# Issuing the additions of x to finished batches two blocks earlier in a bidirectional WKV and binary FFN kernel

## The chip, the cores and the metric

The kernel runs on one core of one Trainium2 chip. Its time is device microseconds for one execution. The kernel before takes 489.81 us, the median of three runs (489.59 to 489.88). The core has a matrix engine (TensorE, PE in the profile, with its weight loads as PEld), a vector engine (VectorE, DVE), an activation engine (ScalarE, ACT), a general engine (GpSimd, POOL) and a queue engine (SyncE, SP) that issues most transfers. Each engine works through its own list of instructions in order; semaphores make one engine wait for another, or for a transfer.

## The reference

For four batches of 1024 time steps and 1024 channels, with `x` as the gate input and one tensor `kv` as both key and value:

```python
tf    = sigmoid(sum(time_emb))                    # one scalar per batch
decay = exp(-exp(w)) * (0.5 + 0.5 * tf)
ek, ekv = exp(min(k, 30)), exp(min(k, 30)) * k
nf, df = scan over time of (a = a*decay + ekv, b = b*decay + ek)
nb, db = the same scan in reverse
euk = exp(min(u + k, 30))
num, den = nf + nb - ekv + euk*k, df + db - ek + euk
y   = sigmoid(x) * num / max(den, 1e-8) * (0.8 + 0.2 * tf)
bw  = where(weight >= 0, 1, -1) * mean(abs(weight), axis=1)
out = x + y @ bw.T + bias
```

The last line is what this case is about: the product is 1024 by 1024 by 1024 for each batch, and `x` is added to it at the very end.

## The kernel before

The work is cut into 32 **blocks**, `g = 0 .. 31`. Block `g` is batch `g // 8` and the 128 channels `g % 8`, over all 1024 time steps, with channels on the 128 partitions (transposed there by the PE, L266 and L272). A block costs VectorE a fixed list: two scans forward (L366), two backward (L379), the numerator's terms (L350), the own terms (L356), the denominator (L389) and a Newton step with the gate (L423). GpSimd floors and clamps the denominator (L396, L346), and multiplies the quotient together (L416, L419, L428); ScalarE takes exponentials and logarithms, and splits the result in a high part (L433) whose remainder GpSimd computes (L438). The own terms are added to the numerator by an accumulating transfer that GpSimd issues (L384).

When the eight blocks of a batch are done, the batch is contracted with the signs of the weight. For batches 0 to 2 the output comes in 16 **groups** `q`, each one half of the time steps (`h`, 512 rows) and one block of 128 output channels: `q = 16 b + 8 h + oc`. A group is 16 matmuls (L449), is scaled and biased by ScalarE (L461), turned back by the PE (L469), copied to a staging tile (L557) and stored to the output in pairs of groups by SP (L135). The groups of a batch are spread over the blocks of the next batch: for batch 0, two groups in each of the blocks 9 to 16; for batches 1 and 2, from blocks 16 and 24 on, five half groups per block. The last batch is contracted differently after the last block, with its rows on the partitions, and `x` is added there by VectorE (L539, L541, L531).

So for batches 0 to 2 the stored output still lacks `x`. The function `add_x(b, n)` (L137) supplies it: GpSimd issues one transfer of 256 rows by 1024 columns (1 MB) from `x` to the output, with an addition at the destination (L140). There are four per batch, `n = 0 .. 3`. Those with `n` 0 and 1 lie in the first half of the time steps, those with `n` 2 and 3 in the second. An addition may only be issued when the four stores of its half have landed, and the framework puts semaphore waits for these stores ahead of it on GpSimd's list; it finds a wait needless for the second addition of a half.

The order of everything is written out by hand in the loop over `g`. Within one block the lines that matter are, in this order: loads by SP (L679 to L686); the denominator of the block before by VectorE, the own-numerator transfer by GpSimd, and then the additions of that block,

```python
            if g > 0:
                dve_denominator(g - 1)
                dma_own_numerator(g - 1)
            for i in adds[g]:
                add_x(*i)
```

and later GpSimd's floor (L707), its clamp (L710), the remainders (L712), `den_product` (L724), `num_product` (L750), VectorE's `dve_newton_gate` (L762, the line L423), which reads what `den_product` (L416) wrote, and GpSimd's `gated_product` (L764). In a block with an addition, ScalarE's logarithm is placed after the edge of the numerator (L721) instead of before it (L709). Additions that are due at 32 are issued behind the last block (L795).

Of the kernel before, what the change touches and what calls it, by code (L numbers as in the profile page):

```python
# [21 lines left out]
def kernel(  # L22
# [32 lines left out]
    NC = C // P  # L55
# [505 lines left out]
    steps = B * NC  # L561
# [36 lines left out]
    fill(g + 2, 0, pieces(range(q + 5, q + groups)))  # L598


    adds = {g: [] for g in range(steps + 1)}
    for b in range(B - 1):
        for n in range(NT // 2):
            adds[min((b + 2) * NC + 2 * n, steps)].append((b, n))

# [9 lines left out]
    with tc.manual_schedule():  # L617
# [57 lines left out]
        for g in range(steps):  # L675
            b, cc = divmod(g, NC)
# [163 lines left out]
        n = NT - 1  # L840
# [41 lines left out]
```

## Time and profile before

| | |
|---|---|
| median of three runs | 489.81 us |
| the profiled execution's own time | 489.83 us |
| its span in the profile | 488.0 us |
| VectorE busy | 474.9 us (97%) |
| GpSimd busy | 402.2 us (82%) |
| PE busy | 363.9 us (75%) |
| ScalarE busy | 335.9 us (69%) |
| transfers of `add_x` | 12 of 1024 KB, median 11.8 us from issue to landing |
| stores of pairs of groups | 24 of 512 KB, median 5.1 us from issue to landing |

Times in the profile count from the start of the span. In a timeline, each line gives start, duration, engine, line of the kernel, operation, what is written and read, and in brackets how long the engine stood idle before it and what ended that. The queue rows (SPq, POOLq) are instructions that a sequencer handles itself. Block `g` is taken to begin with VectorE's L389; block 14 begins at 195.26, block 16 at 222.25, block 18 at 249.30, and the last one, 31, at 425.41.

### The profile page before, as it was taken

Reading aid. Unit: us, or ns where it says so; the run is one execution under the profiler, and the core shown is the slowest. Engines: PE = TensorE matmul, PEld = TensorE weight load, DVE = VectorE, ACT = ScalarE, POOL = GpSimd, SP = SyncE. Lnnn points to the kernel's source line nnn. Section 1 sums busy time; section 2 is a strip of 40 time slices with the busy share of each in tenths; the row PEclk is TensorE's granted clock in tenths of the full one; section 3 lists DMA queues with packets and bytes.
Section 4 is the critical chain, followed back from the end, with each engine's and each line's share of the span. In section 5 each row is a group of like instructions: output and inputs, shape, how many; then the busy total and the mean of one; then the engine's idle time right before and its main releaser. Section 6 shows DMA issues by size and latency. Waiting matters only on the chain.

```text
span 488.0 us, 5214 instructions
## 1 busy us (share of the span) xinstructions
PE 363.9 (75%) x1813; PEld 296.9 (61%) x1813; DVE 474.9 (97%) x331; ACT 335.9 (69%) x466; POOL 402.2 (82%) x276
## 2 busy tenths in 40 slices
PE   3434433344588877778999998965999998989996
PEld 2333332233466666656777777744888777868885
DVE  6999999999999999999999999999999999999976
ACT  4795968869595967769697879697866979724000
POOL 3379999999999999999999999999999999991000
PEclk9975566666699999999999999985999999999999
DMA  8865565555455555559787996889569697899954
GB/s 227 246 173 146 156 174 141 137 141 140 112 147 150 147 141 139 147 139 254 177 208 161 264 235 173 167 213 221 126 108 277 151 271 213 188 229 284 235 198 176
DMA packets 89762, 89.49 MB, mean 183 GB/s; under 512 B 2660, under 2 KB 80776, under 8 KB 88200
## 3 DMA queue, kind: packets, MB, share of 16 engines
q1 hardware_dynamic: 83320, 59.78, 41.0%
q0 software_dynamic: 6400, 29.37, 31.6%
q8 instruction: 14, 0.23, 0.2%
q14 instruction: 12, 0.10, 0.1%
q10 hardware_dynamic: 16, 0.00, 0.0%
HBM read 55.59 MB, written 29.36 MB: 174 GB/s over the span
## 4 chain that ended last, share of the span: by engine, by line
DVE 75%; PE 17%; issue 3%; ACT 2%; POOL 0%; DMA 0%; SPq 0%; DVEq 0%; POOLq 0%; ACTq 0%
DVE num L379 13%; DVE den L379 13%; DVE den L366 13%; DVE num L366 12%; PE wide L517 8%; DVE den L389 7%; DVE num L350 6%; DVE den L423 6%; PE po L449 5%; DVE euk L356 4%; PE last L517 2%; PE bank L517 1%; PE sgT L272 1%; PE turned L469 1%; PE kT L266 1%
## 5 line engine op out<-in xcount | busy, mean ns | idle before, releaser
L449 PE MATMUL po<-gated,wT 128*128 128x512 f32 x768 | 199.7, 408 | 0.3 <-ACT staged L557 0.3
L449 PEld LDWEIGHTS po<-gated,wT 128*128 128x128 f32 x768 | 141.9, 192 | 30.4 <-ACT staged L557 0.8
L266 PE MATMUL kT<-ident,k_rows 128*128 128x128 f32 x248 | 42.1, 325 | 61.6 <-issue 43.0
L272 PE MATMUL sgT<-ident,sg_rows 128*128 128x128 f32 x256 | 43.2, 324 | 46.4 <-DVE den L423 41.2
L438 POOL TENSOR_TENSOR gated<-num,gated 128x512 fp32r<-128x512 f32 x60 | 75.6, 1280 | 2.4
L266 PEld LDWEIGHTS kT<-ident,k_rows 128*128 128x128 f32 x248 | 33.8, 167 | 69.4 <-issue 51.6
L379 DVE TENSOR_TENSOR_SCAN den<-bank,edge_den,den 128x1024 f32<-128x1024 f32 x32 | 74.8, 2339 | 0.4 <-ACT edge_den L372 0.4
L416 POOL TENSOR_TENSOR den<-den,eu 128x1024 f32<-128x1024 f32 x31 | 73.8, 2380 | 1.4 <-ACT eu L411 1.4
L379 DVE TENSOR_TENSOR_SCAN num<-bank,edge_num,num 128x1024 f32<-128x1024 f32 x32 | 74.8, 2337 | 0.0
L419 POOL TENSOR_TENSOR num<-num,eu 128x1024 f32<-128x1024 f32 x31 | 73.7, 2377 | 0.8 <-DMA num<-euk 0.8
L428 POOL TENSOR_TENSOR num<-den,num 128x1024 f32<-128x1024 f32 x30 | 71.8, 2393 | 2.8 <-DVE den L423 0.5
L366 DVE TENSOR_TENSOR_SCAN den<-bank,den 128x1024 f32<-128x1024 f32 x32 | 72.2, 2258 | 0.0
L366 DVE TENSOR_TENSOR_SCAN num<-bank,num 128x1024 f32<-128x1024 f32 x31 | 70.6, 2277 | 0.0
L272 PEld LDWEIGHTS sgT<-ident,sg_rows 128*128 128x128 f32 x256 | 35.1, 167 | 57.1 <-DVE den L423 29.7
L433 ACT CAST gated<-num 128x512 fp32r<-128x512 f32 x64 | 36.5, 618 | 30.2 <-POOL num L428 25.8
L396 POOL TENSOR_SCALAR den<-den,floor 128x1024 f32<-128x1024 f32 x31 | 36.8, 1188 | 20.7 <-DVE den L389 17.5
L404 ACT ACTIVATE eu<-den,gain 128x1024 f32<-128x1024 f32 (+1 forms) x33 | 36.9, 1121 | 20.8 <-POOL den L396 20.4
L517 PE MATMUL wide<-wT,gated 128*128 128x512 f32 x192 | 45.4, 393 | 2.1 <-POOL gated L438 2.1
L557 ACT COPY staged<-turned 128x512 f32<-128x512 f32 x48 | 27.5, 574 | 21.3 <-PE turned L469 21.3
L517 PEld LDWEIGHTS wide<-wT,gated 128*128 128x128 f32 x192 | 35.8, 188 | 10.2 <-POOL gated L438 2.5
L389 DVE SCALAR_TENSOR_TENSOR den<-eu,top,den 128x1024 f32<-128x1024 f32 (+1 forms) x33 | 41.5, 1260 | 0.0
L356 DVE SCALAR_TENSOR_TENSOR euk<-eu,top,kT 128x1024 f32<-128x1024 f32 x31 | 38.7, 1250 | 0.0
(91 smaller groups left out, 578.9 us busy)
## 6 DMA issues: line engine op xcount, KB each, us to landing
sg_rows<-in_x_dram SPq DMA_DIRECT2D x32, 512.0 KB, 5.9
num<-euk POOLq DMA_DIRECT2D x32, 512.0 KB, 5.6
k_rows<-in_fside_BxSxS_dram SPq DMA_DIRECT2D x31, 512.0 KB, 5.2
out_dram<-staged SPq DMA_DIRECT2D x24, 512.0 KB, 5.1
out_dram<-in_x_dram POOLq DMA_DIRECT2D x12, 1024.0 KB, 11.8
w_rows<-in_L_ffn_weight_dram SPq DMA_DIRECT2D x8, 512.0 KB, 5.7
x_rows<-in_x_dram SPq DMA_DIRECT2D x8, 512.0 KB, 11.5
out_dram<-x_rows SPq DMA_DIRECT2D x7, 512.0 KB, 2.6
```

What stands on the lines that cost most here:

```text
L266: nc.tensor.transpose(kT[:, s * P : (s + 1) * P], k_rows[g][:, s, :], ident)
L272: nc.tensor.transpose(t[:, s * P : (s + 1) * P], sg_rows[g][:, s, :], ident)
L356: nc.vector.scalar_tensor_tensor(euk, eus[g], top[:, b, cc : cc + 1], k_ps[g], ALU.min, ALU.mult)
L366: nc.vector.tensor_tensor_scan(t, decay_row(g), t, 0.0, ALU.mult, ALU.add)
L379: nc.vector.tensor_tensor_scan(back, decay_row(g), back, inits[g, which], ALU.mult, ALU.add)
L389: nc.vector.scalar_tensor_tensor(dens[g][:, ts], eus[g][:, ts], top[:, b, cc : cc + 1], dens[g][:, ts], ALU.min, ALU.add,)
L416: engine.tensor_mul(dens[g][:, ts], dens[g][:, ts], eus[g][:, ts])
L419: engine.tensor_mul(nums[g][:, ts], nums[g][:, ts], eus[g][:, ts])
L428: engine.tensor_mul(nums[g][:, ts], dens[g][:, ts], nums[g][:, ts])
L438: engine.tensor_sub(t[:, 1, :], nums[g][:, h * H : (h + 1) * H], t[:, 0, :].bitcast(F32))
L449: nc.tensor.matmul(prods[q], wT[:, cc, oc * P : (oc + 1) * P], gated[b, cc, h][:, i, :], start=(cc == 0 and i == 0), stop=(cc == NC - 1 an ...
L517: nc.tensor.matmul(t, gated[last, cc, h][:, i, s * P : (s + 1) * P], wT[:, cc, cols], start=(cc == 0 and i == 0), stop=(cc == NC - 1 and i ...
```

## The change

Each `add_x` is due two blocks earlier. The due block was `8 (b + 2) + 2 n`, at most 32; it becomes `8 (b + 2) + 2 n - 2`, at most 32:

```diff
     adds = {g: [] for g in range(steps + 1)}
     for b in range(B - 1):
         for n in range(NT // 2):
-            adds[min((b + 2) * NC + 2 * n, steps)].append((b, n))
+            adds[min((b + 2) * NC + 2 * n - 2, steps)].append((b, n))
```

Written out, with `(b, n)` at each block:

| block | 14 | 16 | 18 | 20 | 22 | 24 | 26 | 28 | 30 | after 31 |
|---|---|---|---|---|---|---|---|---|---|---|
| before | – | 0,0 | 0,1 | 0,2 | 0,3 | 1,0 | 1,1 | 1,2 | 1,3 | 2,0 2,1 2,2 2,3 |
| changed | 0,0 | 0,1 | 0,2 | 0,3 | 1,0 | 1,1 | 1,2 | 1,3 | 2,0 | 2,1 2,2 2,3 |

Blocks 16 to 30 have one addition each in both kernels, though of other rows; block 14 gets one that it did not have, and with it the later place of ScalarE's logarithm; three remain after the last block, where there were four. The waits for stores go with `n = 0` and `n = 2` of batches 0 and 1, as before; for batch 2 they now stand ahead of the addition in block 30 and of the second of the three at the end. The lists of the PE and of SP are the same in both kernels, in order and in waits on the stores and loads; VectorE's order is the same too.

## The prediction

> **What bounds the kernel now.** I read the page's busy times first, then the chain that ended last, then the timeline of VectorE and GpSimd in the blocks that the change touches, then the store rows of SP with their time to landing, and last the busy times in windows of the end. The page and, of it, the chain:
>
> ```profile
> span 488.0 us, 5214 instructions
> ...
> PE 363.9 (75%) x1813; PEld 296.9 (61%) x1813; DVE 474.9 (97%) x331; ACT 335.9 (69%) x466; POOL 402.2 (82%) x276
> ...
> DVE 75%; PE 17%; issue 3%; ACT 2%; POOL 0%; DMA 0%; SPq 0%; DVEq 0%; POOLq 0%; ACTq 0%
> ```
>
> VectorE carries three quarters of the chain and GpSimd none. VectorE runs without a gap from block to block: L389, which opens a block, stands at 181.76, 195.26, 208.76, 222.25, 235.75, 249.30, 262.85. A block without an addition takes 13.50 us. So a change to GpSimd's list counts only where it makes VectorE wait. Here is GpSimd in block 14, which has no addition now, and in blocks 16 and 18, which have one, with VectorE's L389, L366 and L423 of block 18 beside it (start, duration, engine, line):
>
> ```profile
> 195.16 0.88 POOL L384 DMA_DIRECT2D num<-euk  x1
> 196.73 1.11 POOL L396 TENSOR_SCALAR den<-den,floor 128x1024 f32<-128x1024 f32 x1 [0.69 <-DVE den L389]
> 201.52 2.40 POOL L416 TENSOR_TENSOR den<-den,eu 128x1024 f32<-128x1024 f32 x1
> 204.27 1.19 DVE L423 SCALAR_TENSOR_TENSOR den<-den,sgT 128x1024 f32<-128x1024 f32 x1
> ...
> 228.80 2.40 POOL L416 TENSOR_TENSOR den<-den,eu 128x1024 f32<-128x1024 f32 x1
> 231.26 1.19 DVE L423 SCALAR_TENSOR_TENSOR den<-den,sgT 128x1024 f32<-128x1024 f32 x1
> ...
> 249.28 0.87 POOL L384 DMA_DIRECT2D num<-euk  x1
> 249.30 1.27 DVE L389 SCALAR_TENSOR_TENSOR den<-eu,top,den 128x1024 f32<-128x1024 f32 x1
> 249.88 1.18 POOL L140 DMA_DIRECT2D out_dram<-in_x_dram  x1
> 250.76 1.46 POOL L396 TENSOR_SCALAR den<-den,floor 128x1024 f32<-128x1024 f32 x1
> 255.92 2.39 POOL L416 TENSOR_TENSOR den<-den,eu 128x1024 f32<-128x1024 f32 x1
> 256.13 2.26 DVE L366 TENSOR_TENSOR_SCAN den<-bank,den 128x1024 f32<-128x1024 f32 x1
> 258.34 1.22 DVE L423 SCALAR_TENSOR_TENSOR den<-den,sgT 128x1024 f32<-128x1024 f32 x1
> ```
>
> The reader is to see how little room there is between L416, which GpSimd writes, and L423, which reads it. Without an addition L416 ends at 203.92 and L423 starts at 204.27: 0.35 us of slack. With one it ends at 231.20 against 231.26, and at 258.31 against 258.34: nothing is left, though VectorE does not yet stand (its L366 ends at 258.39). In a block with an addition, whatever delays GpSimd further delays VectorE by as much, and that time is lost for good.
>
> Now the stores for which the moved additions wait. First the rows of the stores of q = 6 and q = 14, the last ones of the two halves of batch 0, and under each its time from issue to landing, asked for alone. Between the second pair stands what the queues for instruction code moved in 245.7 to 251:
>
> ```profile
> 191.68 0.38 SPq L135 DMA_DIRECT2D out_dram<-staged  x1
> DMA to landing us min/median/max: 3.6/3.6/3.6
> ...
> 245.72 0.38 SPq L135 DMA_DIRECT2D out_dram<-staged  x1
> q8 instruction: 1, 0.02, 1.1%
> DMA to landing us min/median/max: 5.1/5.1/5.1
> ```
>
> The first lands at 195.3, the second at 250.8. Two more stores with the same two loads behind them (178.19, 205.18) land in 3.6; the one at 218.67, with a packet of instruction code beside it, takes 4.8. So 5.1 looks like 3.6 plus a straggler behind a code packet.
>
> **The change, part by part.** *Block 14 gets an addition.* GpSimd would reach it where block 16 has it now, 0.51 us into the block: 195.77. Its store has landed at 195.3, so there is no wait, with 0.5 us to spare. The issue costs GpSimd nothing up to the floor, which waits for L389 in any case (0.69 us idle in block 14; 1.47 us into the block in both 14 and 16). The floor then takes 1.39 instead of 1.11, and L416 ends 0.29 later, inside the 0.35 of slack. What is left is small: blocks 16 and 17, the first pair with an addition, take 13.50 and 13.55 against 13.50 and 13.49 for 14 and 15; L389 at 235.75 takes 1.32 for 1.28 where GpSimd's late L428 runs beside it. Cost 0.06 us; ends 0 and 0.15 (blocks 18 and 19 take 13.55 and 13.59). The own-numerator transfer ahead of it lands in 6.9 instead of 5.8 as in block 16, at about 202, before L419 reads it at 203.9. ScalarE's logarithm moves behind the edge of the numerator as in block 16, where the chain reaches L416 in time.
>
> *The addition of the second half, from block 20 to 18.* It inherits the wait for the store issued at 245.72. GpSimd gets there at 249.88; the store lands at 250.81. The nearest row for what follows is the end of the trace, where GpSimd waits for a transfer issued at 425.64 that takes 10.1, so lands at 435.74, and starts at 435.83: 0.09 later. The addition then starts at 250.90, 1.02 later than now. Behind it stand the floor, the clamp, both remainders and L416, and behind those ScalarE's logarithm and VectorE's L423. Not all of 1.02 reaches them. An issue right behind another one takes 1.18, one that stands alone 0.88 (the first of the four at 438.17); the floor that overlaps its end takes 1.46 and ends 1.16 after it. So: 250.90 + 0.88 + 1.15 = 252.93 for the floor's end, which is now at 252.22. That is 0.71, and with no slack at L416, VectorE stands 0.71. Ends: 0 if the store lands in 3.6 (249.32, ahead of 249.88), and 1.02 if the whole shift comes through; with the slowest store of the middle blocks, 6.6 us, the addition starts at 252.41, the floor ends at 254.44, and it is 2.22. I take 0.71, since the trace has this very store at this place, SP's list is unchanged, and both the store and GpSimd shift alike by the 0.06 of block 14.
>
> *Two other waits that come with the move:* the addition 1,0 in block 22 needs the store of 286.35, which lands in 3.6, and is due at 304; 1,2 in block 26 (due 358.2) needs the store of 327.04, 2.9; 2,0 in block 30 (due 412.4) needs a store issued before 387 that takes at most 11.7. All have landed: cost nothing, and the cover is over 10 us. Blocks 16 to 30 otherwise keep one issue and 1 MB each. GpSimd's own-numerator transfers, which the additions are moved past, keep their places; no store on SP waits for an addition.
>
> *One addition less at the end.* Four issues take 3.45 us from 438.17, three would take about 2.85, and the DMA engines lose 1 MB there. Nothing waits behind them on GpSimd, which ends there. The last one lands by about 467, and the span ends at 488. The windows (PE, PEld, DVE, ACT, POOL, clock, DMA share, GB/s) say what the end is bound by:
>
> ```profile
> 438.00:452.00 14.00, 14.00 (x65) 11.52 (x64) 13.18 (x21) 5.86 (x9) 3.62 (x5) 1.00 1.01 274
> 452.00:470.00 18.00, 18.00 (x80) 14.80 (x79) 14.46 (x21) 0.00 (x0) 0.00 (x0) 1.00 0.91 229
> ```
>
> The DMA engines are full (1.01), but the PE is busy in all 32 us, and no instruction that touches the rows of x idles for a transfer. Gain 0; at the other end, if one issue did count, 0.6.
>
> Sum: 489.83 (the profiled execution's time, 0.02 above the median of the runs) + 0.06 + 0.71 = 490.60 us.
>
> [...] The trace has both, 3.6 and 5.1, and for this store 5.1.
>
> **The rivals.** *No wait at all.* The straggler is not there, and the store lands in 3.6 as three others do. For it: the margin is then 0.56. Against: the code packet belongs to an instruction list that does not change. Time 489.83 + 0.06 = 489.89, the same.
>
> *The whole shift comes through, or several semaphores are seen one after another.* The wait is for four stores, so four waits stand on GpSimd's list; if what follows starts only after the full issue, 1.02 plus up to 0.15 in blocks 14 and 15 gives 489.83 + 1.02 + 0.15 = 491.0, slower. It decides from a delay of 0.92 on, since the bound is 0.98. Against it: the floor waits for L389 anyway and has room to close up.
>
> *A late store.* The store at 245.72 takes 6.6 instead of 5.1, as those at 256.89 and after 310 do beside an addition's transfer: 489.83 + 0.06 + 2.22 = 492.1, slower by 0.5%. Against: the addition of block 16 has landed by about 234, so nothing of the kind runs at 245.
>
> *The end gets shorter,* if the last phase hangs on the full DMA engines: one issue, 0.6 us, gives 489.3; a quarter of the 27.1 us that the slowest addition takes to land is 6.8, and 483 the extreme. Against: PE without a gap for 32 us.
>
> **How the numbers follow.** The forecast, 490.3 to 490.8: 0.41. No wait, 489.75 to 490.1: 0.15. Whole shift, 490.8 to 491.3: 0.25. Late store, above 491.3: 0.12. Shorter end: 0.07, of which 0.06 below 488.85. A difference under 0.2% (0.98 us) is about what a measurement of this kernel can't tell from no change. Slower takes the whole shift and the late store, 0.37, and 0.01 of the forecast's upper edge; faster 0.06; the same 0.56. The range leaves out the shorter end and most of the late store: 489.7 to 491.5.
>
> **What would show it.** Right: in block 18 GpSimd idle some 0.8 to 1.0 us ahead of L140 or of the floor, VectorE idle about 0.7 us ahead of L423, ended by L416; block 18 near 14.2 us, all others as now; the rest of the trace shifted by 0.8. Block 14: L416 ending 0.3 later, L423 in its place. Wrong: block 18 at 13.55 with the store landed by 249.8 (no wait); a wait in block 14 too, if its store takes over 4.1; or an end that is more than 0.3 us shorter from VectorE's last L423 on. The prediction would be most wrong if the store's straggler moves, as its size decides the sum.

## The result, and the profile after

The changed kernel takes 491.54 us, the median of seven runs (490.78 to 493.36). The kernel before, run beside it, takes 489.81 (489.59 to 489.94, seven runs). The ratio is 1.0046, with an interval from 1.003 to 1.0061. So the change costs time, and more than the 490.60 of the forecast: the median lies just above the range's upper end of 491.5. Four executions in the comparisons further down took 915 us or more, the traced one of no_wait among them, and are left out of every count and row there.

The profiled execution took 491.54 us, with a span of 489.8, which is 1.8 more than before. The page of the kernel after (the span, the busy times, the chain of work that ended last):

```profile
span 489.8 us, 5214 instructions
...
PE 364.5 (74%) x1813; PEld 297.3 (61%) x1813; DVE 474.8 (97%) x331; ACT 336.3 (69%) x466; POOL 402.2 (82%) x276
...
DVE 71%; PE 18%; POOL 4%; issue 4%; ACT 2%; DMA 0%; SPq 0%; POOLq 0%; DVEq 0%; ACTq 0%
```

The busy times of VectorE and GpSimd have not moved. In the chain, GpSimd, which had no share, now has 4%, taken from VectorE: somewhere VectorE has waited for GpSimd. The timeline of the kernel after says where. First GpSimd in block 14, with VectorE's L423 (start, duration, engine and line), then block 18, with the next block's L389:

```profile
195.72 1.16 POOL L140 DMA_DIRECT2D out_dram<-in_x_dram  x1
196.66 1.39 POOL L396 TENSOR_SCALAR den<-den,floor 128x1024 f32<-128x1024 f32 x1
201.74 2.41 POOL L416 TENSOR_TENSOR den<-den,eu 128x1024 f32<-128x1024 f32 x1
204.21 1.20 DVE L423 SCALAR_TENSOR_TENSOR den<-den,sgT 128x1024 f32<-128x1024 f32 x1
...
250.52 0.85 POOL L140 DMA_DIRECT2D out_dram<-in_x_dram  x1 [0.40 <-issue]
251.13 1.41 POOL L396 TENSOR_SCALAR den<-den,floor 128x1024 f32<-128x1024 f32 x1
256.24 2.39 POOL L416 TENSOR_TENSOR den<-den,eu 128x1024 f32<-128x1024 f32 x1
258.67 1.22 DVE L423 SCALAR_TENSOR_TENSOR den<-den,sgT 128x1024 f32<-128x1024 f32 x1 [0.27 <-POOL den L416]
263.18 1.36 DVE L389 SCALAR_TENSOR_TENSOR den<-eu,top,den 128x1024 f32<-128x1024 f32 x1
```

In block 14 the addition has no wait, and L423 follows L416 (which ends at 204.15) without idle time. In block 18 VectorE stands idle 0.27 us ahead of L423, ended by L416, and the next block begins at 263.18 where it began at 262.85: the loss of 0.33 is where the forecast put it, and smaller than its 0.71. By block 31 no more than 0.15 is left of all this (L389 at 425.56 against 425.41). The other 1.6 us come afterwards, and they begin on PE. PE at the end of the kernel after (timeline, the same columns):

```profile
430.76 0.96 PE L517 MATMUL wide<-wT,gated 128*128 128x512 f32 x3 [2.10 <-POOL gated L438]
...
432.01 7.26 PE L517 MATMUL wide<-wT,gated 128*128 128x512 f32 x24
439.11 1.03 PE L272 MATMUL sgT<-ident,sg_rows 128*128 128x128 f32 x8
```

And of the kernel before:

```profile
430.62 0.96 PE L517 MATMUL wide<-wT,gated 128*128 128x512 f32 x3 [2.10 <-POOL gated L438]
...
431.87 5.66 PE L517 MATMUL wide<-wT,gated 128*128 128x512 f32 x24
```

The same 24 matmuls take 7.26 instead of 5.66. The windows say why (stretch and length, busy time of PE, PEld, VectorE, ScalarE and GpSimd with their counts, then the granted clock, the DMA share and GB/s). After:

```profile
428.90:432.30 3.40, 1.54 (x7) 1.29 (x8) 3.40 (x3) 1.74 (x3) 3.32 (x4) 1.00 0.90 259
432.30:435.70 3.40, 3.40 (x10) 2.63 (x9) 3.40 (x3) 0.30 (x1) 2.80 (x2) 0.50 0.90 241
```

Before:

```profile
429.20:432.60 3.40, 1.99 (x9) 1.66 (x10) 3.40 (x3) 1.29 (x3) 3.32 (x4) 1.00 0.96 264
432.60:436.10 3.50, 3.50 (x17) 2.88 (x16) 3.50 (x3) 0.29 (x1) 2.65 (x3) 1.00 0.89 226
```

PE's clock is halved for 3.4 us after the change, and not before. So one profiled pair shows two causes, the foreseen wait at 0.3 us and a clock at 1.6. The experiments separate them, and find how large each is over many runs.

### The profile page after: what moved, and what is told of

It is laid out like the page before. It is cut to its first block, busy times and chain, and to the rows that moved or that the text cites. A ratio compares the mean times of both kernels' runs of the same rounds, so it can differ in the third digit from the quotient of the medians.

```text
span 489.8 us, 5214 instructions
## 1 busy us (share of the span) xinstructions
PE 364.5 (74%) x1813; PEld 297.3 (61%) x1813; DVE 474.8 (97%) x331; ACT 336.3 (69%) x466; POOL 402.2 (82%) x276
## 4 chain that ended last, share of the span: by engine, by line
DVE 71%; PE 18%; POOL 4%; issue 4%; ACT 2%; DMA 0%; SPq 0%; POOLq 0%; DVEq 0%; ACTq 0%
DVE den L379 12%; DVE num L379 12%; DVE den L366 12%; DVE num L366 11%; PE wide L517 8%; DVE den L389 6%; DVE num L350 6%; DVE den L423 6%; PE po L449 5%; DVE euk L356 3%; PE last L517 2%; POOL gated L438 1%; POOL den L416 1%; PE bank L517 1%; POOL den L396 1%
## 5 line engine op out<-in xcount | busy, mean ns | idle before, releaser
L438 POOL TENSOR_TENSOR gated<-num,gated 128x512 fp32r<-128x512 f32 x60 | 75.7, 1280 | 2.4
L416 POOL TENSOR_TENSOR den<-den,eu 128x1024 f32<-128x1024 f32 x31 | 73.7, 2379 | 1.4 <-ACT eu L411 1.4
L419 POOL TENSOR_TENSOR num<-num,eu 128x1024 f32<-128x1024 f32 x31 | 73.7, 2376 | 0.7 <-DMA num<-euk 0.7
L428 POOL TENSOR_TENSOR num<-den,num 128x1024 f32<-128x1024 f32 x30 | 71.9, 2395 | 2.8 <-DVE den L423 0.5
L404 ACT ACTIVATE eu<-den,gain 128x1024 f32<-128x1024 f32 (+1 forms) x33 | 36.9, 1120 | 20.2 <-POOL den L396 20.1
L517 PE MATMUL wide<-wT,gated 128*128 128x512 f32 x192 | 47.0, 403 | 2.1 <-POOL gated L438 2.1
L517 PEld LDWEIGHTS wide<-wT,gated 128*128 128x128 f32 x192 | 37.0, 194 | 10.6 <-POOL gated L438 2.5
L389 DVE SCALAR_TENSOR_TENSOR den<-eu,top,den 128x1024 f32<-128x1024 f32 (+1 forms) x33 | 41.4, 1259 | 0.0
```

The costliest lines, as they stand in the source:

```text
L389: nc.vector.scalar_tensor_tensor(dens[g][:, ts], eus[g][:, ts], top[:, b, cc : cc + 1], dens[g][:, ts], ALU.min, ALU.add,)
L416: engine.tensor_mul(dens[g][:, ts], dens[g][:, ts], eus[g][:, ts])
L419: engine.tensor_mul(nums[g][:, ts], nums[g][:, ts], eus[g][:, ts])
L428: engine.tensor_mul(nums[g][:, ts], dens[g][:, ts], nums[g][:, ts])
L438: engine.tensor_sub(t[:, 1, :], nums[g][:, h * H : (h + 1) * H], t[:, 0, :].bitcast(F32))
L517: nc.tensor.matmul(t, gated[last, cc, h][:, i, s * P : (s + 1) * P], wT[:, cc, cols], start=(cc == 0 and i == 0), stop=(cc == NC - 1 and i ...
```

## The experiments

**The two kernels again, and each half of the change alone.** The theory: the loss is the wait for the store in block 18 and varies with the store's landing; the half clock has to do with PE's idle time and not with the change. A rival: the moved transfers disturb the end, or block 14 or the three at the end cost something. Four kernels, run side by side: both kernels unchanged; *wait_alone*, the kernel before with nothing but the addition 0,2 brought to block 18 (and 0,1 put into block 20 in its place):

```diff
 (kernel before, after the loop that fills adds)
+    adds[18], adds[20] = adds[20], adds[18]
```

and *no_wait*, the changed kernel with an addition in block 18 that has nothing to wait for:

```diff
 (kernel after, after the loop that fills adds)
+    adds[18] = [(0, 1)]
```

> The kernel before, unchanged, for a second trace. Clock theory (the loss of the changed kernel is mostly the TensorE clock, granted at 0.5 for 3.4 us right after the PE has idled 2.1 us in block 31): the clock stays at 1.00 from 340 us to the end, and the PE's 24 matmuls after that idle take 5.7 us. Wait theory (the loss is VectorE standing in block 18 for the store of q = 14): says nothing of this kernel. Both: 489.8 us, spread under 0.4 us. If the place of the 3.4 us clock windows against the start of the program were left to chance, some of these runs would show the drop too, and be 1.6 us longer.

> The changed kernel, unchanged, for a second trace and more times. Wait theory: 490.8 to 493.4 us again, and the excess of the traced run stands between VectorE's L366 and L423 of block 18. Clock theory: the excess of the traced run stands in the PE from 432 us on, with the clock at 0.5 for 3.4 us, about 1.6 us; block 18 gives 0.3 to 1.

> The kernel before with the additions of blocks 18 and 20 exchanged: 0,2 in block 18, as in the changed kernel, 0,1 in block 20. It has the wait for the fresh store and nothing else of the change: no addition in block 14, four at the end. Wait theory: the whole loss, 491.5 us with the same spread. Clock theory: 0.3 to 0.7 from block 18 alone, 490.1 to 490.5, unless the delay in block 18 is itself what brings the drop at 432 us.

> The changed kernel with 0,1 issued a second time in block 18 in place of 0,2, so that what stands there waits for nothing fresh. Rows 256 to 511 of batch 0 get x twice and rows 512 to 767 never; all else is the changed kernel: an addition in block 14, three at the end. Wait theory: the loss is gone, 489.9 us. Clock theory: the clock drop at 432 us and 1.6 us stay, 491.4 us, unless the delay in block 18 brings the drop.

Measured, against 34 runs of the kernel before that they share (the means are over all of these runs):

| kernel | its runs | ratio to before |
|---|---|---|
| before, the shared runs | 13 at 489.66 to 490.25, 21 at 491.16 to 491.64, mean 490.76 | |
| before_again | 5 at 489.70 to 490.02, 7 at 491.12 to 491.44 | 0.9999 (0.9986 to 1.0012) |
| after_again | 490.69 to 493.28, mean 491.76 | 1.0019 (1.0006 to 1.0033) |
| wait_alone | 489.72 to 493.02, mean 491.42 | 1.0017 (1.0001 to 1.0033) |
| no_wait | 5 at 489.79 to 489.90, 5 at 491.22 to 491.49, one 492.06 | 1.0002 (0.9987 to 1.0017) |

The unchanged kernel before has two levels 1.5 us apart, with nothing between. Its profile beside them fell in the upper one; the windows of before_again, and its 24 matmuls from the timeline:

```profile
428.10:431.50 3.40, 1.29 (x6) 0.80 (x5) 3.40 (x3) 2.34 (x3) 3.31 (x3) 1.00 0.92 260
431.50:434.90 3.40, 3.40 (x10) 2.60 (x9) 3.40 (x3) 0.29 (x1) 3.37 (x3) 0.50 1.01 269
```

```profile
432.11 6.99 PE L517 MATMUL wide<-wT,gated 128*128 128x512 f32 x24
```

It is the half clock at the same place, so the change is not needed for it: 21 of 34 runs of a kernel without the change lie at the upper level, 1.5 us higher. The wait is made by the change. Wait_alone has it, and so has after_again; no_wait, whose addition has nothing to wait for, has times that lie like those of before. Here is the timeline of after_again in block 18; in this execution the 24 matmuls behind PE's idle time take 5.67 us, so the half clock has no part in it there:

```profile
251.90 0.86 POOL L140 DMA_DIRECT2D out_dram<-in_x_dram  x1 [1.61 <-DMA out_dram<-staged]
252.51 1.42 POOL L396 TENSOR_SCALAR den<-den,floor 128x1024 f32<-128x1024 f32 x1
257.64 2.39 POOL L416 TENSOR_TENSOR den<-den,eu 128x1024 f32<-128x1024 f32 x1
260.06 1.22 DVE L423 SCALAR_TENSOR_TENSOR den<-den,sgT 128x1024 f32<-128x1024 f32 x1 [1.52 <-POOL den L416]
```

And of wait_alone, whose span of 489.1 us is 1.1 above that of before, less than the 1.6 of the half clock:

```profile
251.35 0.87 POOL L140 DMA_DIRECT2D out_dram<-in_x_dram  x1 [1.23 <-DMA out_dram<-staged]
...
259.52 1.22 DVE L423 SCALAR_TENSOR_TENSOR den<-den,sgT 128x1024 f32<-128x1024 f32 x1 [1.15 <-POOL den L416]
```

GpSimd names the store as what it waited for, and VectorE stands 1.52 and 1.15 us. The size goes with the store: it took 4.1 us to land in the recorded profile, 5.0 in wait_alone and 5.4 in after_again. The rows of the addition's line alone, in after and in after_again, show what comes between the landing and the transfer's start (count, duration min/median/max in ns, first and last start):

```profile
L140 POOLq EVENT_SEMAPHORE  x2: 17/30/43, 249.9 to 250.0; - x2
L140 POOL DMA_DIRECT2D out_dram<-in_x_dram x1: 855/855/855, 250.5 to 250.5; - x1
```

```profile
L140 POOLq EVENT_SEMAPHORE  x2: 17/30/43, 251.3 to 251.3; - x2
L140 POOL DMA_DIRECT2D out_dram<-in_x_dram x1: 857/857/857, 251.9 to 251.9; - x1
```

The semaphores are seen as the store lands, and the issue begins 0.6 us later.

**PE's idle time filled.** PE stands 2.1 us in block 31, between 428.5 and 430.6, waiting for GpSimd's L438. The theory: this idle time makes the half clock, when it falls badly against the grid of 3.4 us on which the clock changes; so a PE that is given work there keeps its clock, and the wait can then be measured without that noise. A rival: the two levels have another cause, and remain. To fill it, the last block's product 2,0 is made twice: first in the old place in a copy with its own open and close, whose sums are thrown away, and again after GpSimd's remainders, where PE used to stand.

```diff
             if final:
-                pe_wide_product(2, 0, range(NC - 3))
+                open_wide(2, 0)
+                for c in range(NC - 3):
+                    for i in range(2):
+                        nc.tensor.matmul(
+                            wide[2, 0],
+                            gated[last, c, 0][:, i, 2 * P : 3 * P],
+                            wT[:, c, columns(0)],
+                            start=(c == 0 and i == 0),
+                            stop=(c == NC - 4 and i == 1),
+                        )
...
             if final:
+                pe_wide_product(2, 0, range(NC - 3))
                 for i in ((1, 0), (1, 1), (2, 0)):
```

before_filled is the kernel before with this, after_filled the kernel after with it.

> The kernel before, with the first ten matmuls of one product of the last block (rows 256 to 383 of the last batch, first half of the columns) made twice, so that the PE works through the 2.1 us in block 31 in which it waits for the remainders. Clock theory as it stands now (that idle time, if enough of it falls into one 3.4 us window, halves the clock in the next window, in either kernel): the upper group of times, 491.2 to 491.5, is gone, and all lie at 489.8 to 490.2, with the clock at 1.00 from 345 us to the end. If the drop has another cause, two groups 1.5 us apart remain.

> The same filling in the changed kernel. What is then left of the spread is the wait alone. Wait theory, with the hand-over that the traces show (0.65 us from the landing of the store of q = 14 to the start of the addition, 2.03 from there to the end of the floor): 0 to 0.1 where the store takes 3.6 us, 0.3 at 4.1, 1.2 at 5.0, 1.55 at 5.4, so times from 489.9 to 491.8 in one broad group and a mean near 491.0. Against it: if the wait mattered only through the clock, these times would be those of the filled kernel before.

Measured, beside 35 runs of the kernel before (14 at the lower level, mean 489.88, 21 at the upper one, mean 491.51): before_filled 489.66 to 490.07 in 11 of 12 runs and 490.73 in one, mean 489.93, ratio 0.998 (0.9969 to 0.9991). After_filled 490.06 to 491.66, mean 490.97, ratio 1.0001 (0.9988 to 1.0014). The windows and the timeline of before_filled:

```profile
428.40:431.80 3.40, 3.40 (x16) 2.62 (x15) 3.40 (x3) 2.12 (x3) 3.32 (x3) 1.00 1.00 265
431.80:435.20 3.40, 3.40 (x17) 2.78 (x16) 3.40 (x3) 0.30 (x1) 3.23 (x3) 1.00 0.98 265
```

```profile
428.13 2.45 PE L517 MATMUL wide_t<-wT,gated 128*128 128x512 f32 x10
...
431.93 5.66 PE L517 MATMUL wide<-wT,gated 128*128 128x512 f32 x24
```

PE now has work through the gap, the clock is 1.0 there, the 24 matmuls take 5.66, and the upper level is gone. Ten matmuls whose sums nobody reads make the kernel before 0.93 us faster in the mean. Between the two filled kernels the change costs 1.05 us (0.70 to 1.36, by resampling the runs). The trace of after_filled has a store of 5.4 us and VectorE idle for 1.54:

```profile
251.80 0.86 POOL L140 DMA_DIRECT2D out_dram<-in_x_dram  x1 [1.59 <-DMA out_dram<-staged]
...
259.99 1.22 DVE L423 SCALAR_TENSOR_TENSOR den<-den,sgT 128x1024 f32<-128x1024 f32 x1 [1.54 <-POOL den L416]
```

**The wait taken out of the filled kernel.** With the fill, block 14 and the end can be held apart from the wait to a few tenths: after_filled with the edit of no_wait.

> As no_wait (0,1 a second time in block 18 in place of 0,2; rows 256 to 511 of batch 0 get x twice, rows 512 to 767 never), with the filling of the PE, so that the clock leaves one group of times. What the rest of the change costs, an addition in block 14 and three at the end instead of four: 0.06 by the sum on record, so 489.9 to 490.0 in the mean, against 489.93 of the filled kernel before. If the end or block 14 matter more: 0.3 or more off that.

Measured: 489.73 to 489.93, median 489.80, ratio 0.9984 (0.9974 to 0.9994). That is 0.12 below before_filled (0.30 below to 0.01 above), and after_filled is 1.17 above it (0.85 to 1.45). This kernel and one_later were measured in a later comparison than the other filled ones; the lower level of before has a mean of 489.85 there and of 489.88 in theirs, so the differences can be off by some hundredths for that reason. The store of no_wait_filled landed as late as any, in 5.4 us, and nobody waited. The timeline of no_wait_filled:

```profile
249.87 1.17 POOL L140 DMA_DIRECT2D out_dram<-in_x_dram  x1
...
258.34 1.22 DVE L423 SCALAR_TENSOR_TENSOR den<-den,sgT 128x1024 f32<-128x1024 f32 x1
```

So the addition in block 14, the other moved additions and the three at the end together cost nothing that these runs can see, and the wait costs all of it.

**The code packet moved away from the store.** The forecast read the 5.1 us of this store as 3.6 plus a straggler behind a packet of instruction code. To move that packet, PE's list is made longer ahead of it: the gate's transposes of blocks 3 to 6 are made twice in after_filled, 64 instructions more.

```diff
 (kernel after_filled, at the end of a block)
+            if 3 <= g <= 6:
+                for s in range(NT):
+                    nc.tensor.transpose(
+                        sg_ps[g][:, s * P : (s + 1) * P], sg_rows[g][:, s, :], ident
+                    )
```

> The filled changed kernel with the eight transposes of the gate made twice in blocks 3 to 6, where the PE is idle two thirds of the time: 64 more instructions of the PE ahead, so that its code packet of block 17 is fetched some 6 us earlier, ahead of the store of q = 14. If the straggler behind the code packet makes the store late: it lands in 3.6 us, VectorE stands 0.1 us or less in block 18, and the time is that of the filled kernel before, 489.8 to 490.2. If the store is late for another reason: 490.3 to 491.8 as in the filled changed kernel.

Measured: six runs at 489.80 to 490.34 and six at 491.04 to 492.29, mean 490.82, ratio 0.9999 (0.9983 to 1.0014). The profiled execution, 489.89 us, has no code packet between 244 and 252 us, where before has one of 0.02 MB that starts at 248.5; the store lands in 3.6, and VectorE does not wait. The store's landing and the addition's row in code_moved:

```profile
DMA to landing us min/median/max: 3.6/3.6/3.6
```

```profile
250.14 1.04 POOL L140 DMA_DIRECT2D out_dram<-in_x_dram  x1
```

That half of the runs lost time all the same was not expected. So two more traces of the same kernel were taken.

> The kernel code_moved once more, for a trace: half of its times lay at 489.8 to 490.3 and half at 491.0 to 492.3, and the trace so far is of the lower half. If the code packet is what makes the store late, the store lands in 3.6 us in this trace too, whatever the time, and the time of the upper half is lost in another place. If not, a run of the upper half shows a store of 5 us or more with no code packet beside it.

> The kernel code_moved a third time, with the same question: does a trace of the upper half of its times show the store of q = 14 landing late, or the time lost in another place.

The first of these took 490.03 us, the second 491.02. In both the store lands in 3.6 and block 18 has no wait. The second loses its time at the end, where VectorE waits for the last block's own-numerator transfer (the timeline of code_moved_3):

```profile
444.46 0.69 DVE L419 TENSOR_TENSOR num<-num,eu 128x512 f32<-128x512 f32 x1 [1.98 <-DMA num<-euk]
```

That transfer took 10.3 us, where it took 5.1 in code_moved_2 and 8.1 in code_moved; in the ten traces without this edit it took 5.2 to 5.9. So three traces out of three without the packet have the store at 3.6, and ten out of ten with it have 3.9 to 5.4. The same traces show it at two other stores, once in each direction. The store of 178.2 took 3.6 in before and after_filled, and 5.1, 4.9 and 4.8 in the three traces of code_moved, which have a packet beside it. The store of 218.7 took 4.8 and 5.2 in before and after_filled, with a packet beside it, and 3.6 in all three of code_moved, without one. The packet makes the store late, and a prompt store takes the wait away; but this kernel as a whole is no faster in the mean. Its 64 instructions move the later packets too, and the transfer at its end was late only in traces with them, two of three; what held it is open.

**The addition issued later in the same or the next block.** If only the wait costs, the addition 0,2 can be put behind the work that VectorE needs: in after_filled behind L416 of block 18 (behind_product), or in block 19 (one_later).

```diff
 (behind_product)
                 for i in adds[g]:
-                    add_x(*i)
+                    if g != 18:
+                        add_x(*i)
...
                 den_product(g - 1)
+                if g == 18:
+                    add_x(0, 2)

 (one_later, after the loop that fills adds)
+    adds[19], adds[18] = adds[18], []
```

> The filled changed kernel with the addition 0,2 still in block 18, but issued by GpSimd behind the product that VectorE's L423 waits for (L416) and not ahead of the floor; ScalarE's order is kept. By then (near 258 us) the store has landed for 7 us, so there is no wait; the issue, 0.6 to 0.9 us, is no longer hidden under the wait for L389, and L419, L428 and the next floor come that much later. Wait theory: the loss of 0.3 to 1.8 is gone, and 0 to 0.3 for the issue comes back in block 19: 489.9 to 490.4. If an addition in block 18 costs by its traffic and not by its wait: 490.3 to 491.8 again.

> The filled changed kernel with the addition 0,2 in block 19 in place of 18: still one block ahead of the kernel before, but 17 us after the store of q = 14 was issued. ScalarE's logarithm goes back to its early place in block 18 and to the late one in 19. Wait theory: no wait, so the 1.0 us between the filled kernels is gone, 489.9; since blocks 19 and 20 now both have an addition and GpSimd cannot catch up its 0.3 us in between, 0 to 0.5 comes back: 489.9 to 490.4, in one narrow group. If the loss came from the early addition itself: near 491.0.

Both are compared with before_filled. Behind_product took 490.67 to 491.25, mean 490.91, ratio 0.9996 (0.9986 to 1.0006): 0.98 above before_filled (0.79 to 1.14), so nothing was won, and the expectation was missed. The wait at L423 is gone, but another stands in its place. The timeline of behind_product around the start of block 19:

```profile
258.27 0.88 POOL L140 DMA_DIRECT2D out_dram<-in_x_dram  x1
...
261.64 2.39 POOL L428 TENSOR_TENSOR num<-den,num 128x1024 f32<-128x1024 f32 x1
...
262.88 2.23 DVE L389 SCALAR_TENSOR_TENSOR den<-eu,top,den 128x1024 f32<-128x1024 f32 x1
```

The same two in the kernel before:

```profile
260.73 2.40 POOL L428 TENSOR_TENSOR num<-den,num 128x1024 f32<-128x1024 f32 x1
...
262.85 1.36 DVE L389 SCALAR_TENSOR_TENSOR den<-eu,top,den 128x1024 f32<-128x1024 f32 x1
```

The addition pushes L428 back by 0.91. L389 starts as before (262.88 and 262.85) but takes 2.23 us instead of 1.36. In both kernels it ends 1.08 after L428 does (265.11 and 264.03; 264.21 and 263.13), though they overlap for 1.15 in one and for 0.28 in the other. L389 takes 1.27 in block 18 of before, where the two overlap by 0.03. So about 0.2 us of it is done when L428 ends (an estimate, 1.27 less 1.08), however long they overlap; what holds it until then these rows do not show.

One_later took 490.14 to 490.86, mean 490.48, ratio 0.9993 (0.9983 to 1.0003): 0.56 above before_filled (0.34 to 0.75). Its addition waits for nothing, but a block without an addition has the logarithm in its earlier place, and block 18 now is one. ScalarE and VectorE in block 18 of one_later:

```profile
253.27 1.16 ACT L404 ACTIVATE eu<-den,gain 128x1024 f32<-128x1024 f32 x1
254.32 0.28 ACT L372 ACTIVATE edge_num<-num,edge 128x1 f32<-128x1 f32 x1
...
254.64 2.35 DVE L379 TENSOR_TENSOR_SCAN num<-bank,edge_num,num 128x1024 f32<-128x1024 f32 x1 [0.62 <-ACT edge_num L372]
```

The logarithm (L404) stands ahead of the edge (L372), and VectorE waits 0.62 for the edge. The same two in block 18 of the kernel before, in the other order, without a wait:

```profile
253.19 0.30 ACT L372 ACTIVATE edge_num<-num,edge 128x1 f32<-128x1 f32 x1
253.39 1.14 ACT L404 ACTIVATE eu<-den,gain 128x1024 f32<-128x1024 f32 x1
...
253.87 2.34 DVE L379 TENSOR_TENSOR_SCAN num<-bank,edge_num,num 128x1024 f32<-128x1024 f32 x1
```

That is the loss, by another path. The early place alone is not enough for it: block 17 of before has the logarithm there too, and VectorE does not wait. In block 17 the logarithm begins 2.66 us into the block (238.41). In block 18 it begins 3.90 us into the block, since ScalarE is busy from a table load at 249.79 on without a gap. The median, 490.49, also lies a little above the 490.4 that was expected.

## Why the prediction was right and wrong

*Block 14.* Forecast 0.06, from blocks that already had an addition. In the recorded profile blocks 14 and 15 together take 27.06 (195.19 to 222.25) against 26.99: 0.07, and VectorE does not wait. Right, but the 0.5 us to spare were not there. In after the wait for the store of 191.6 ends at 195.2 and the addition starts at 195.72, which is as late as it would start behind the own-numerator transfer of 195.11 in any case. The hand-over described next uses up the whole margin; it costs nothing here, since the floor waits for L389 anyway.

*The additions of batches 1 and 2, and the end.* Forecast 0 for both. No_wait_filled, which has the other moves and three additions at the end, is as fast as before_filled (0.12 below, interval over zero). Right; the shorter end, the rival that would have made the kernel faster, did not come.

*The wait in block 18.* The mechanism and place were right: the store of 245.72 is waited for, and GpSimd's lateness reaches L423 in full (in after, L416 starts 0.32 later than in before, and L423 0.33). The size was not. The first step that failed is "starts at 435.83: 0.09 later". That row was a multiplication (L419) waiting for a transfer. What waits here is the issue of a transfer, and the traces give 0.6 for it: semaphores first seen at 249.9, 250.7, 251.3 and 251.2 in after, wait_alone, after_again and after_filled, issues at 250.52, 251.35, 251.90 and 251.80. Where nothing is waited for, the addition's issue starts 0.60 us behind the one ahead of it in any case (249.28 and 249.88 in before, and so in each of its eight blocks with an addition), so the hand-over does not show. A nearer row stood in the trace of before: at 14.06 an issue of L384 is ended by a wait for VectorE's scan, 0.31 us after the scan's end. No issue there is ended by a wait for a landing. The next step, 0.88 and then 1.15 to the floor's end, was right: 2.02 to 2.04 in these traces. With 0.6 in place of 0.09 and the store at its 5.1, the forecast's own sum would be 1.2 for the wait instead of 0.71, and 491.1 in all, which is inside its range. The runs measure 1.05 and 1.17 in the mean.

*The store.* It was taken at 5.1, with 3.6 and 6.6 as ends. It landed in 3.9 to 5.4 in the ten traces with the packet beside it, and the wait of VectorE is 0.27 to 1.54 in the four traces that have one. In the recorded profile it took 4.1, 1.0 less than forecast, which outweighs the 0.5 that the hand-over was short; so the wait there is 0.27 and not 0.71, by the luck of one execution. The late store of 6.6 is in no trace; the slowest runs, above 492.9, were not traced. Without the packet it took 3.6. Of the rivals, the whole shift (a delay of 1.02, 491.0) came nearest to the cost that the comparisons give, but for another reason than it gave: the two semaphore rows last 0.06 together, and the floor does close up behind the issue.

*The rest of the trace.* The second step that failed is "all others as now; the rest of the trace shifted by 0.8", and it is the one that carried the recorded time out of the range. Of PE the prediction says only that it is busy without a gap in the 32 us from 438 on. Its gap lies just ahead of them, 2.1 us in block 31, and the sum had no term for what the clock does after it. In the profiled execution the trace is shifted by 0.15 at block 31, and then 24 matmuls take 7.26 us instead of 5.66 at half clock: 1.6 of the 1.8 us. The kernel before lies at its upper level, 1.4 to 1.6 us higher, in 54 of its 91 runs in the three comparisons of the experiments.

The recorded means are 2.23 apart (492.03 and 489.80). The change accounts for 1.0 to 1.2 of it: 1.00 by after_again against before, 1.05 by the filled kernels, 1.17 by after_filled against no_wait_filled. Wait_alone gives less, 0.66 by the means, but its interval, 0.05 to 1.6, contains these. An estimate for the remaining 1.0 to 1.2 is a half clock in some five of the seven runs after (5/7 of 1.6 is 1.14); only one of the seven was traced, so this is not shown. That the half clock struck in none of the seven runs of before there is hard to put down to chance: at 54 in 91, none in seven has odds of about 1 in 500. Why it did not strike there is open. So the change truly costs about 1 us or 0.2%, and the recorded 0.46% contains a lottery that the kernel before had too. That the median lies only 0.04 above the range is luck and no support for the sum: in the profiled execution the foreseen wait was 0.27, and most of the loss was the one that was not foreseen.

## What to carry to other kernels

When the issue of a transfer is moved up until it waits for a landing, count from the landing and add the hand-over, 0.6 us here, and ask whether the first engine behind it has any slack: here it had 0.03 us, so nearly all of it came through. Before comparing kernels at a few tenths of a per cent, look at the granted clock around each idle stretch of PE ahead of a part that PE bounds; here a repeated product that nobody reads was worth 0.93 us, about as much as the change under study cost. And in a schedule without slack, moving a piece of work away from one wait can put it on the next: three places for one addition cost 1.05, 0.98 and 0.56 us, by three different waits.

## What the hardware did that was not expected

**The clock.** The granted clock changes on a grid of 3.41 us: in the traces of before and after, each recorded stretch at one clock that ends inside the span lasts a whole number of these steps (3.41, 6.83, 10.24, 13.65, 92.16 and 191.15 us). The grid's place against the start of the program differs between executions: its borders near PE's idle time are at 429.2 and 432.6 in before (counted on in steps of 3.41 us from the clock's last change, at 340.5), 428.9 and 432.3 in after, 428.1 and 431.5 in before_again. Where PE was busy 1.54 (after) or 1.29 us (before_again) of a window's 3.4 us, the next window had half the clock; where it was busy 1.99 (before), not. Two other windows of the same grid lie between: PE was busy 1.59 from 210.4 to 213.8 in after and 1.66 from 183.5 to 186.9 in before, and the clock was 1.00 in the window behind each. These rows are from 140 us on, with the clock at 1.00. How far they hold earlier is open: from 20 to 60 us, with PE busy 17.45 us, the profile of before gives a clock of 0.67; the mean over the whole execution is 0.901 there and 0.982 in the traced one of wait_alone. With the same idle time (2.10 us in before, 2.11 in before_again), the 24 matmuls behind it took 5.66 us in the one and 6.99 in the other, whose borders fall 1.1 us earlier; with the idle time filled, they took 5.66 (before_filled).

**The hand-over.** A transfer that GpSimd issues after a wait for a store starts 0.6 us after its semaphores are first seen, in each of the four traces in which VectorE waits for it (249.9 to 250.52, 250.7 to 251.35, 251.3 to 251.90, 251.2 to 251.80), and also in code_moved (249.5 to 250.14), where VectorE does not.

**A code packet and a store.** With one packet of instruction code of 0.02 MB beside it, the 512 KB store of 245.7 landed in 3.9 to 5.4 us (ten traces), and without it in 3.6 (three traces), the same store in the same place. Not every packet cost as much: the store of 272.9 in before, with a packet 0.4 us after its issue, took 3.8. What sets the size was not shown.
